# Where the last block of an MLP folds in the running maxima of the next image's scores

## The chip, the cores and the metric

One core of one Trainium2 chip runs the whole program in one launch. The metric is the device time of one execution in microseconds, median of the runs shown. Its engines are TensorE (PE in the profile; PEld is its weight load), VectorE (DVE), ScalarE (ACT), GpSimd (POOL) and SyncE (SP), each with its own instruction stream in order; they meet through semaphores.

## The reference

Four images of 256 channels by 64 x 64 pixels, all in fp32, pass through two layers. The first is an attention over the 4096 pixels of an image:

```python
q = jnp.einsum('oc,bcn->bno', wq, xf) + bq
k = jnp.einsum('oc,bcn->bon', wk, xf) + bk[None, :, None]
attn = jax.nn.softmax(jnp.einsum('bnd,bdm->bnm', q, k), axis=-1)
v = jnp.einsum('oc,bcn->bon', wv, xf) + bv[None, :, None]
out = jnp.einsum('bcn,bmn->bcm', v, attn).reshape(B, Cc, H, W)
return gamma[0] * out + x
```

The second normalizes the result, adds the output of a small clustering step, normalizes again, adds an MLP (256 to 1024 channels, tanh-GELU, back to 256), and ends in a channel scale and a 256 x 256 pointwise convolution, each with batch norm and ReLU.

## The kernel before

The order of instructions is the order of the Python calls: `tc.manual_schedule()` keeps each engine's stream as written, and the framework adds only the semaphore waits that data and buffers need. The four images run one after another, and each goes through `weighting` (the attention's sums, about half a thousand microseconds), `cluster`, and `mlp`. The beginning of the next image's attention is woven into the present image's `cluster` and `mlp`.

**Scores of the next image.** A block of attention is 512 query pixels. Its scores are made in eight units of 512 keys, `score(u)` at L351: four matmuls of 32 rows each (L364) write two PSUM halves, two ScalarE copies (L372 and L373) put them into an SBUF tile `s`, and the softmax needs the maximum over all of it. For the units made inside the MLP the maxima are not recorded on the spot. `score` appends them to a list, `maxima`, as four closures (unit 0: two), each of which records one VectorE instruction when it is called, L377: `top = max(top, s quarter)`, 128 x 512. The first two of a unit read what L372 copied, the other two what L373 copied.

**The MLP's blocks.** `mlp` walks over eight blocks of 512 pixels (seven for the third image, whose eighth block is done later by `late_block`). Each block has four steps, `j` = 0 to 3, one for each pair of 128-channel groups of the hidden layer. A step is one call of `first`, which calls `seven`: seven half-size products instead of eight, in three groups of PSUM banks, `hp`, `hq` and `hr` (all L1377), with additions on VectorE (L1368, through `plus`), one ScalarE copy (L1385) and four GELUs (L1332). The banks come from a pool of two, so a group reuses the bank of the group but one before it, once that has been read. Between these products TensorE does the second layer's products of the step before, `mo`: L1294 in all blocks but the last, and L1278 in the last, where `end` is true. `slots` says how many of them go at each of four places.

In the last block, VectorE also finishes the block before it: three additions L1436 to L1438 and updates of `x` at L1423, some of them called from `plus` through the list `drips`. ScalarE's two ReLUs L1414 follow, then GpSimd's L1222, and TensorE's pointwise products `pw` at L1233 in step 2. The helper `rest()` takes one closure out of `maxima`, if there is one, and records it; in every block it is called ahead of and behind `first` in steps 2 and 3. The table `at` places the score units: unit 6 behind step 3 of the last block but one and unit 7 behind step 2 of the last; for the third image, units 6 and 7 behind steps 1 and 2 of the last block.

**Behind the last block** comes the handover:

```python
        for _ in range(2):
            next(todo)
        if nxt:
            while maxima:
                rest()
            nxt.fold(0)
            nxt.maximum()
        table(AF.Exp)
        for _ in todo:
            pass
        if nxt:
            nxt.first()
```

Two `mo` products of step 3 are recorded; all maxima that are left are recorded; `fold` (L394) reduces `top` to one row of 512; `maximum` calls `across`, where TensorE transposes `top` (`tt`, L400), VectorE takes the row maxima (L402) and spreads them on a diagonal (`dg`, L404). Then the other two `mo` products follow, `first` spreads the maxima over PSUM with a matmul by ones (`mb`, L453), `finish` and `last` complete the block (L1423, L1414, `pw`), and the exponentials (L465, L468) and sums (`av`, L478) of the next image start. The fourth image has no next one, and its list is empty.

Of the kernel before, what the change touches and what calls it, by code (L numbers as in the profile page):

```python
# [45 lines left out]
def attention_then_cluster_block(  # L46
# [1114 lines left out]
    def mlp(b, ys, stats2, fill, nxt, blocks, turned, maxima):  # L1161
# [26 lines left out]
        def norm(nb, eng):  # L1188


            pairs[nb] = pr = spool.tile([P, 2, KC, NB], F32, tag="s", name=f"xn2_{b}_{nb}")

            def scaled(k):
                nc.vector.tensor_scalar(
                    pr[:, 0, k, :],
                    block(ys, k, nb),
                    ga[:, k : k + 1],
                    gb[:, k : k + 1],
                    ALU.mult,
                    ALU.add,  # L1200
                )

            def parts():
                rest = factors(eng, pr[:, 0], pr[:, 1])
                scaled(0)
                if nb == 0:
                    next(rest)
                scaled(1)
                yield
                yield from rest  # L1210

            rest = parts()
            next(rest)
            return rest
# [4 lines left out]
        def last(nb, beside, eng):  # L1219

            zs = pairs.pop(nb)
            eng.tensor_tensor(zs[:, 0, 1], zs[:, 1, 0], zs[:, 1, 1], ALU.subtract)  # L1222

            if beside:
                ps = [
                    ps_m.tile([P, NB], F32, tag="m", name=f"pw{c}_{b}_{nb}") for c in range(KC)
                ]
            else:
                two = ps_s.tile([P, 2, NB], F32, tag="s", name=f"pw_{b}_{nb}")
                ps = [two[:, c, :] for c in range(KC)]  # L1230
            for c in range(KC):
                for k in range(KC):
                    nc.tensor.matmul(  # L1233
                        ps[c],
                        pw_q[2 * k + c],
                        zs[:, 0, 1] if k and c else zs[:, 1, k],
                        start=(k == 0),
                        stop=(k == KC - 1),
                    )
            for c in range(KC):  # L1240
                rectified(c, zs[:, 0, c], ps[c])
                leave(nb, c, zs[:, 0, c])

        def rectified(c, o_s, src):
            nc.scalar.activation(
                o_s, src, AF.Relu, scale=pw_s[:, c : c + 1], bias=pw_e[:, c : c + 1]
            )

        def leave(nb, c, o_s):
            nc.sync.dma_start(out=ob[:, c, nb * NB : (nb + 1) * NB], in_=o_s)  # L1250

        def factors(eng, src, dst):


            e, f, g, h = quarters(src)
            t2, t4, t3, _ = quarters(dst)
            yield eng.tensor_tensor(f, f, e, ALU.subtract)
            yield eng.tensor_tensor(t2, h, f, ALU.subtract)
            yield eng.tensor_tensor(t3, e, t2, ALU.subtract)
            yield eng.tensor_tensor(t4, t2, g, ALU.subtract)  # L1260
# [65 lines left out]
        def first(nb, j, todo, slots, meanwhile=lambda: None):  # L1326


            hs = work.tile([P, 2, NB], F32, tag=("t", "acc")[j % 2], bufs=1, name=f"hs_{b}_{nb}_{j}")

            def gelu(i, src):
                nc.scalar.activation(  # L1332
                    src, src, AF.Gelu_apprx_tanh, bias=pvc("b1", P, j + 4 * (i > 1))
                )

            ws = [
                w[:, j * P : (j + 1) * P] for w in (W_A, w_abcd, W_CD, w_bac, w_bcd, W_B, W_D)
            ]
            seven(f"{nb}_{j}", ws, pairs[nb][:, 0], pairs[nb][:, 1], quarters(hs), gelu, todo, slots, meanwhile)
            return hs  # L1340
# [71 lines left out]
        def finish(nb, acc):  # L1412
            def relu(c):
                nc.scalar.activation(  # L1414
                    pairs[nb][:, 1, c, :],
                    block(ys, c, nb),
                    AF.Relu,
                    scale=dw_d[:, c : c + 1],
                    bias=dw_e[:, c : c + 1],
                )  # L1420

            def scaled(y, term, c):
                nc.vector.scalar_tensor_tensor(y, term, par("ls2", c), y, ALU.mult, ALU.add)  # L1423

            if len(acc) == KC:
                for c in range(KC):
                    scaled(block(ys, c, nb), acc[c], c)
                    relu(c)
                return

            _, _, z, w = acc
            p7, p5, p6, p4 = (t[:, i * HB : (i + 1) * HB] for t in (z, w) for i in range(2))
            own = pairs[nb][:, 1]
            d1, d2, d3, d4 = quarters(own)
            y0, y1 = block(ys, 0, nb), block(ys, 1, nb)
            nc.vector.tensor_tensor(d4, p6, d1, ALU.add)  # L1436
            nc.vector.tensor_tensor(d3, p7, d4, ALU.add)
            nc.vector.tensor_tensor(d2, p5, d4, ALU.add)  # L1438
            scaled(y1[:, HB:], p5, 1)
            scaled(y1[:, :HB], p4, 1)  # L1440
            drips.append(lambda: scaled(y0, own[:, 0], 0))
            drips.extend([lambda: None] * 3)
            drips.append(
                lambda: scaled(
                    y1.rearrange("p (x n) -> p x n", x=2),
                    d3.unsqueeze(1).to_broadcast([P, 2, HB]),
                    1,
                )
            )
            hooks.append(lambda: relu(0))  # L1450
            return lambda: relu(1)
# [9 lines left out]
        def rest():  # L1461
            if maxima:
                maxima.pop(0)()
# [8 lines left out]
        for nb in range(blocks):  # L1472
            end = nb == blocks - 1
            for j in range(4):
                if j > 1:
                    rest()
                pw = (lambda: last(nb - 1, True, nc.gpsimd)) if end and j == 2 else lambda: None
                hs = first(nb, j, todo, slots, pw)
                if nb == 0 and j == 0:
                    fill(N)  # L1480
                if j > 1:
                    rest()
                if j == 0:
                    if nb:
                        rectify = finish(nb - 1, acc)
                    acc = [
                        ps_a.tile([P, NB], F32, tag=f"a{c}", name=f"mo{c}_{b}_{nb}")
                        for c in range(KC)
                    ]
                    if not end:  # L1490
                        acc += [
                            ps_m.tile([P, NB], F32, tag="m", name=f"mo{c}_{b}_{nb}")
                            for c in range(2, 4)
                        ]
                    elif nxt:

                        nc.sync.dma_start(
                            out=a21_s, in_=w2.rearrange("(k p) m -> p k m", p=P)[:, :h_n, P:]
                        )
                        nxt.q_block(1, nc.sync)  # L1500
                elif j == 1:
                    assert not drips and not hooks
                    if nb:
                        rectify()
                    if not end:
                        ahead = norm(nb + 1, nc.gpsimd)
                        if nb:
                            own = factors(nc.gpsimd, pairs[nb - 1][:, 1], pairs[nb - 1][:, 0])
                        else:
                            own = left_factors()  # L1510
                elif j == 2 and nb and not end:
                    pointwise(nb - 1)
                scored = nxt and (nb, j) in at
                if scored:
                    copies = []
                    nxt.score(at[nb, j], copies, maxima)
                    copies.pop()()
                if len(acc) == KC:
                    todo = second(nb, acc, hs, j)
                    slots = (2, 1, 1, 0) if scored else (0, 1, 1, 2)  # L1520
                else:
                    todo = second_by_seven(nb, acc, hs, j, own, ahead)
                    slots = (0, 2, 2, 3)
                    if scored:
                        slots = (3, 1, 2, 1)
                    elif j == 2 and nb:
                        slots = (3, 1, 0, 3)
# [32 lines left out]
    with tc.manual_schedule():  # L1560
# [3 lines left out]
        for b in range(B):  # L1564
# [11 lines left out]
            stats, cells, rest = here.weighting(ahead, fill, (lambda: None) if b else derived)  # L1576
# [82 lines left out]
```

## Time and profile before

| what | value |
|---|---|
| median of 3 runs | 3349.32 us (3348.83 to 3349.82) |
| profiled execution, its own time | 3348.09 us |
| its span, first to last instruction | 3346.3 us |
| mean granted TensorE clock | 0.997 |
| VectorE busy | 2222.5 us (66%) |
| ScalarE busy | 1681.7 us (50%) |
| GpSimd busy | 1931.9 us (58%) |
| L377, maxima by closures: 120 instructions, median, longest | 0.68 us, 1.21 us |

The span lies 1.8 us under the profiled execution's own time, and that execution 1.2 us under the median. In a timeline row the first number is the start in microseconds from the beginning of the span, the second the length of the group, "x4" the number of instructions that were merged, and the bracket the engine's idle time ahead of it with the instruction that ended it. An fp32 matmul stands as two records, and a record's end is modelled with the pipeline's tail in it, so the next one can start some 0.16 us ahead of that end. Three places of the span matter here, the ends of the first three images' MLPs, at about 880, 1710 and 2513 us.

### The profile page before, as it was taken

To read this page: it belongs to the slowest core of one execution; us is meant where nothing else is said; L and a number is where in the kernel's file an instruction comes from. 1 tells how busy PE (TensorE), PEld (TensorE's weight loads), DVE (VectorE), ACT (ScalarE), POOL (GpSimd) and SP (SyncE) were. 2 spreads that over 40 slices of the span, in tenths; PEclk is the share of its full clock that TensorE was granted. 3 is DMA by queue.
4 is the path that set the end of the run, shared out by engine and by line. 5 is a ranking of instruction groups with operands and counts; after the bars stand their busy time and mean duration, and the time that the engine had idled before them with its cause. 6 is when DMAs were issued, how large, how long until landed. Compare 5 with 4: busy or idle time off the path is not lost.

```text
span 3346.3 us, 34677 instructions
## 1 busy us (share of the span) xinstructions
PE 3301.5 (99%) x12266; PEld 1805.9 (54%) x12266; DVE 2222.5 (66%) x3554; ACT 1681.7 (50%) x2253; POOL 1931.9 (58%) x1366
## 2 busy tenths in 40 slices
PE   8999999999999999999999999999999999999999
PEld 4433444788533344578844334457873343446786
DVE  5667764677666766467766676647766766765675
ACT  5545553545555554355455555435455555544444
POOL 2655666366365676646636566554644676573664
PEclk9999999999999999999999999999999999999999
DMA  2000002000000000200000000010000000010000
GB/s 72 13 13 10 14 9 87 4 13 20 26 12 13 13 13 16 78 4 20 20 23 13 10 13 13 23 71 4 20 26 13 13 13 13 10 40 1 13 20 26
DMA packets 43101, 70.97 MB, mean 21 GB/s; under 512 B 9680, under 2 KB 18480, under 8 KB 42928
## 3 DMA queue, kind: packets, MB, share of 16 engines
q1 hardware_dynamic: 37040, 60.83, 5.5%
q10 hardware_dynamic: 5632, 7.41, 0.9%
q8 instruction: 96, 1.57, 0.2%
q0 software_dynamic: 256, 0.52, 0.1%
q14 instruction: 77, 0.63, 0.1%
HBM read 43.46 MB, written 16.89 MB: 18 GB/s over the span
## 4 chain that ended last, share of the span: by engine, by line
PE 94%; DVE 4%; ACT 1%; POOL 1%; DMA 0%; issue 0%; ACTq 0%; DVEq 0%; POOLq 0%
PE av L478 54%; PE mo L1294 9%; PE sc L364 8%; PE hq L1377 5%; PE hp L1377 3%; PE hr L1377 3%; PE fv L874 3%; PE vp L315 2%; PE mo L1278 1%; PE hq_pw L1377 1%; DVE st L979 1%; PE pw L1233 1%; PE hr_pw L1377 1%; PE hp_pw L1377 1%; DVE x L998 0%; DVE top L377 0%
## 5 line engine op out<-in xcount | busy, mean ns | idle before, releaser
L478 PE MATMUL av<-s,v 128*128 128x512 f32 x4096 | 1819.2, 598 | 0.6 <-ACT s L468 0.6
L473 POOL TENSOR_TENSOR acc<-acc,s 128x1024 f32<-128x1024 f32 x448 | 1057.7, 2361 | 538.4 <-ACT s L468 519.5
L478 PEld LDWEIGHTS av<-s,v 128*128 128x128 f32 x4096 | 759.1, 190 | 1044.7 <-issue 1034.5
L468 ACT ACTIVATE s<-s 128x1024 f32<-128x1024 f32 x512 | 540.1, 1057 | 592.5 <-DVE s L465 549.5
L465 DVE TENSOR_TENSOR s<-s,mb 128x1024 f32<-128x1024 f32 x512 | 595.9, 1206 | 19.0 <-ACT mb L449 16.4
L386 DVE TENSOR_TENSOR top<-sc,top 128x1024 f32<-128x1024 f32 x196 | 239.5, 1222 | 374.7 <-PE sc L364 374.4
L1332 ACT ACTIVATE hs<-hs,pv_s 128x256 f32<-128x256 f32 x496 | 232.4, 502 | 340.7 <-DVE hs L1368 340.7
L1294 PE MATMUL mo<-hs,w 128*128 128x256 f32 x1512 | 387.0, 382 | 0.0
L382 ACT COPY s<-sc 128x1024 f32<-128x1024 f32 x224 | 224.9, 1004 | 225.5 <-PE sc L364 225.5
L1294 PEld LDWEIGHTS mo<-hs,w 128*128 128x128 f32 x1512 | 282.5, 190 | 57.8 <-ACT hs L1332 19.8
L364 PE MATMUL sc<-q,k 32*128 32x512 f32 x2048 | 300.5, 640 | 0.4 <-ACT s L387 0.4
L389 DVE TENSOR_TENSOR top<-sc,top 128x1024 f32<-128x1024 f32 x196 | 240.1, 1225 | 71.9 <-ACT s L382 59.5
L387 ACT COPY s<-sc 128x1024 f32<-128x1024 f32 x224 | 227.1, 1014 | 66.4 <-DVE top L384 36.1
L1368 DVE TENSOR_TENSOR hs<-hq,hs 128x256 f32<-128x256 f32 x496 | 198.8, 422 | 78.3 <-PE hq L1377 68.4
L470 POOL TENSOR_TENSOR acc<-s 128x1024 f32<-128x1024 f32 x32 | 75.3, 2353 | 285.0 <-ACT s L468 285.0
L1301 POOL TENSOR_TENSOR hs<-hs 128x256 f32<-128x256 f32 x108 | 82.3, 762 | 189.2 <-ACT hs L1385 85.1
L364 PEld LDWEIGHTS sc<-q,k 32*128 32x128 f32 x2048 | 86.4, 182 | 183.7 <-issue 123.1
L1368 DVE TENSOR_TENSOR hs<-hp,hs 128x256 f32<-128x256 f32 x124 | 52.2, 421 | 136.5 <-ACT hs L1385 136.5
L315 PE MATMUL vp<-wv_s,x 128*128 128x256 f32 x512 | 127.8, 395 | 1.9 <-ACT v L323 1.5
L1377 PE MATMUL hr<-xn,w 128*128 128x256 f32 x496 | 127.5, 379 | 0.5 <-DVE hs L1368 0.5
L315 PEld LDWEIGHTS vp<-wv_s,x 128*128 128x128 f32 x512 | 95.1, 194 | 30.2 <-issue 12.7
L1377 PEld LDWEIGHTS hr<-xn,w 128*128 128x128 f32 x496 | 94.1, 190 | 19.1 <-issue 4.8
(262 smaller groups left out, 3495.5 us busy)
## 6 DMA issues: line engine op xcount, KB each, us to landing
out<-xn SPq DMA_DIRECT2D x62, 256.0 KB, 2.1
x<-in_x SPq DMA_DIRECT2D x30, 512.0 KB, 6.5
w<-in_w SPq DMA_DIRECT2D x8, 1024.0 KB, 10.2
mr<-row_mx SPq DMA_DIRECT2D x28, 256.0 KB, 3.1
rden<-row_rd SPq DMA_DIRECT2D x28, 256.0 KB, 3.1
q<-q ACTq DMA_DIRECT2D x96, 64.0 KB, 2.0
mix<-in_wfv SPq DMA_DIRECT2D x8, 192.0 KB, 8.1
q<-q SPq DMA_DIRECT2D x24, 64.0 KB, 2.0
```

Of the source, the lines that this page charges most:

```text
L315: nc.tensor.matmul(vps[0][:, i % 2, :], xs[i * P // XT][:, k, o : o + P], wv_s[:, k, :], start=(k == 0), stop=(k == KC - 1),)
L364: nc.tensor.matmul(halves[r // 2][:, r % 2, :], k_s[rows, g, :], q_s[rows, :], start=True, stop=True)
L386: nc.vector.tensor_tensor(top, halves[1], top, ALU.max)
L389: nc.vector.tensor_tensor(top, halves[0], top, ALU.max)
L465: nc.vector.tensor_tensor(sh, sh, mxs[nb].unsqueeze(1).to_broadcast([P, 2, NB]), ALU.subtract)
L468: nc.scalar.activation(sh, sh, AF.Exp)
L473: nc.gpsimd.tensor_tensor(acc, acc, s[:, 2 * h : 2 * h + 2], ALU.add)
L478: nc.tensor.matmul(av[c], own["v"][:, RG * g + quarter, c * P : (c + 1) * P], slots[u][:, quarter, :], start=(g == 0 and quarter == 0), st ...
L1294: return nc.tensor.matmul(bank[:, half * HB : (half + 1) * HB], a[:, j], t, start=start, stop=stop)
L1332: nc.scalar.activation(src, src, AF.Gelu_apprx_tanh, bias=pvc("b1", P, j + 4 * (i > 1)))
L1368: nc.vector.tensor_tensor(dst, ps, term, ALU.add)
L1377: nc.tensor.matmul(out, w, x, start=True, stop=True)
```

## The change

Two edits in the loop over the steps of `mlp`, both for the last block alone (`end`): `rest()` is also called behind `first` in steps 0 and 1, and twice more ahead of `first` in step 3.

```diff
             for j in range(4):
                 if j > 1:
                     rest()
+                if end and j == 3:
+
+                    rest()
+                    rest()
                 pw = (lambda: last(nb - 1, True, nc.gpsimd)) if end and j == 2 else lambda: None
                 hs = first(nb, j, todo, slots, pw)
                 if nb == 0 and j == 0:
                     fill(N)
-                if j > 1:
+                if j > 1 or end:
                     rest()
```

Four more closures are thus taken out of `maxima` ahead of the handover's `while maxima` loop. Lines behind the edits move down by four.

## The prediction

> **What bounds the kernel now.** I read the page first. Its first line and the chain of waits say that TensorE sets the time:
>
> ```profile
> PE 3301.5 (99%) x12266; PEld 1805.9 (54%) x12266; DVE 2222.5 (66%) x3554; ACT 1681.7 (50%) x2253; POOL 1931.9 (58%) x1366
> ...
> PE 94%; DVE 4%; ACT 1%; POOL 1%; DMA 0%; issue 0%; ACTq 0%; DVEq 0%; POOLq 0%
> ```
>
> So an edit to VectorE's order pays only where TensorE stands idle for VectorE, or runs slowly because it stood idle. I then read TensorE's timeline at the ends of the first three images' MLPs. These are the first end and the third; the second equals the first to within 0.02 us (`tt` at 1710.10, idle 1.54):
>
> ```profile
> 877.90 1.98 PE L1278 MATMUL mo<-hs,w 128*128 128x512 f32 x4 [1.06 <-ACT hs L1332]
> 881.43 0.66 PE L400 MATMUL tt<-ident,top 128*128 128x128 f32 x4 [1.54 <-DVE top L394]
> ...
> 2507.90 1.98 PE L1278 MATMUL mo<-hs,w 128*128 128x512 f32 x4 [1.06 <-ACT hs L1332]
> 2513.83 0.66 PE L400 MATMUL tt<-ident,top 128*128 128x128 f32 x4 [3.95 <-DVE top L394]
> 2514.32 2.81 PE L1278 MATMUL mo<-hs,w 128*128 128x512 f32 x4
> ```
>
> The transposes `tt` wait for `fold`, L394: 1.54 us twice and 3.95 us once. VectorE's timeline at the same ends says why: behind the last additions of step 3 stand five maxima (nine for the third image) and then the fold. The last two rows are from step 2 to 3 of the first image:
>
> ```profile
> 877.55 3.09 DVE L377 TENSOR_TENSOR top<-top,s 128x512 f32<-128x512 f32 x5
> 880.68 0.69 DVE L394 TENSOR_TENSOR top<-top 128x512 f32<-128x512 f32 x1
> ...
> 2507.55 5.50 DVE L377 TENSOR_TENSOR top<-top,s 128x512 f32<-128x512 f32 x9
> ...
> 868.11 1.28 DVE L377 TENSOR_TENSOR top<-top,s 128x512 f32<-128x512 f32 x2
> 873.41 0.42 DVE L1368 TENSOR_TENSOR hs<-hp,hs 128x256 f32<-128x256 f32 x1 [4.01 <-ACT hs L1385]
> ```
>
> Ahead of step 3's additions VectorE idles 4.01 us. Last, the granted clock (the number behind POOL's) in short windows:
>
> ```profile
> 640.00:660.00 20.00, 18.52 (x82) 14.62 (x82) 14.18 (x36) 9.61 (x18) 9.80 (x11) 0.91 0.00 1
> ...
> 880.00:884.00 4.00, 2.57 (x9) 1.37 (x10) 3.18 (x6) 0.00 (x0) 0.00 (x0) 1.00 0.00 0
> ...
> 2514.00:2516.00 2.00, 2.00 (x7) 1.04 (x7) 1.44 (x3) 0.00 (x0) 0.00 (x0) 0.78 0.00 0
> 2516.00:2518.00 2.00, 2.00 (x4) 0.89 (x3) 1.35 (x2) 0.85 (x2) 0.00 (x0) 0.50 0.00 0
> 2518.00:2520.00 2.00, 2.00 (x5) 0.81 (x5) 1.20 (x2) 0.78 (x1) 0.00 (x0) 0.86 0.00 0
> ```
>
> After the third end's 3.95 us of idling TensorE worked about 3.4 us at half clock; after the first end's 1.54 us it did not.
>
> **What moves.** Nothing is added or removed: in the built programs only VectorE's order differs, and no other stream, wait or DMA moves. Counting closures (unit 6 leaves four at the start of the last block, unit 5 for the third image):
>
> - first and second image, before: one maximum ahead of step 2, two between steps 2 and 3, five behind step 3. After: one behind step 0, two between 1 and 2, one of unit 6 and three of unit 7 between 2 and 3, one behind step 3.
> - third image, behind step 3: nine before, five after; the three new ones ahead of step 3 are of unit 6.
>
> One more maximum in a row costs (3.09 - 0.68)/4 = 0.60 us, and (5.50 - 3.09)/4 = 0.60 us again.
>
> **Gain at the first two ends.** Four maxima less bring the fold forward by 2.41 us, from 881.37 to 878.96. TensorE's four `mo` records, from 877.90, let the next matmul start after 1.82 us (as in step 2: `mo` at 870.12, `hp` at 871.94), at 879.72. That is later than the fold, so TensorE becomes the limit: `tt` moves from 881.43 to 879.72, a gain of 1.71, not of 2.41. What follows hangs on `tt` (L402, `dg`, `mb`, L1423, L1414, `pw`) and moves with it: 1.7 each. What is late next is the 1.06 us wait for the GELU ahead of these `mo` records, which stays.
>
> **Gain at the third end.** Nine minus five maxima is again 2.41 us; here the fold remains the last to come, so `tt` moves by all of it and idles 1.54, the picture that the first end shows today. From the start of `tt` to the first `av` the first end takes 888.74 - 881.43 = 7.31 us and the third 2522.77 - 2513.83 = 8.94. With idle time shortened to 1.54 the half clock should go, worth 1.63. Here the Trainium skill, "TensorE: Matmul & The Clock Gate", section "Part 1: The HAM clock gate", has a rule: the clock halves after a whole idle window of about 3.4 us, counted freely. By it 1.54 us can't halve the clock, and 1.63 is certain. The trace is less kind: between 640 and 660 us the clock was halved (mean 0.91) where the longest idle piece is 1.44 us, with one-column matmuls around it. So the rule's threshold is too high for this kernel. I still take 1.63, from the nearest rows, two ends with 1.06 and 1.54 us idle at clock 1.00; the other bound, 0, I give a chance. Sum 4.04.
>
> **Cost of the early places.** The maximum behind step 0 falls into a stretch in which VectorE has no gap (852.35 to 859.51), so everything there slips by 0.60: L1436 to L1438, L1423, the additions of step 1, and ScalarE's GELUs and ReLUs behind them.
>
> ```profile
> 852.35 0.76 DVE L1368 TENSOR_TENSOR hs<-hr,hs 128x256 f32<-128x256 f32 x2
> 853.02 0.41 DVE L1436 TENSOR_TENSOR xn<-mo,xn 128x256 f32<-128x256 f32 x1
> ...
> 858.74 0.89 ACT L1332 ACTIVATE hs<-hs,pv_s 128x256 f32<-128x256 f32 x2
> ...
> 860.41 1.27 POOL L1222 TENSOR_TENSOR xn<-xn 128x512 f32<-128x512 f32 x1 [9.98 <-ACT xn L1414]
> ```
>
> Who waits: `mo` at 859.93 reads the GELU of 858.74, which ends at 859.25 and after the slip at 859.85. With some 0.05 for a semaphore its weights load about 0.15 later than now, of which overlap leaves 0.05 on TensorE. `hr` needs the `hp` addition read out: 855.34 before, 855.94 after, weights at 856.06: free by 0.1. L1222 slips to 861.0 and ends by 862.3; its reader is the last pair of the `pw` that starts at 862.94: hidden. The two maxima ahead of step 2 end at 860.7, and the addition behind them, 860.62 now, goes to 861.24 with its copy L1385; the next one waits for `hq` until 862.29 anyway (1.24 idle). For the third image unit 6's `sc` at 2486.99 takes its second half's bank from step 1's `hr` additions, read out at 2486.74, after the slip at 2487.34; that half starts 0.39 later, and TensorE with it, as when the same wait stretched unit 7's `sc` to 2.04 us at 2498.14. Total: 0.05, 0.05, 0.39. Without the slacks of 0.1 to 1.2 named here, each end would lose up to the 0.60.
>
> **Cost of the places ahead of step 3.** VectorE runs in order: a maximum that waits for unit 7's copies holds step 3's additions behind it. The copies L372 and L373 end at 871.28 and 872.20; two maxima start at 871.32, the third at 872.52 and ends at 873.20. The addition behind it starts at 873.41: free by 0.2, and even if late, 1.32 us of idle time ahead of `hq`'s addition covers it. In the third image unit 6 is copied long before; three maxima run from 2499.5 to 2501.4, the addition comes at 2503.41.
>
> A second rule speaks against the change: the skill's "GPSIMD Engine Reference", section "1. Specifications", says that GpSimd shares its SBUF interfaces with VectorE and contends with VectorE instructions with two SBUF inputs, which these maxima are. The trace agrees that they can stretch: one beside L1260 took 0.95, the longest 1.21. By the rule alone four moved maxima at 0.95 would cost 3.8 us of VectorE instead of 2.4. But GpSimd is idle from 850.4 to 860.4 and from 861.7 to 888.3, so I take 0.60.
>
> **Sum.** 1.71 - 0.05 twice, and 4.04 - 0.39: 3.3 + 3.65 = 7.0 us, call it 7.1 with the 0.02 to 0.03 that the unstalled `tt` saves at the first two ends. The profiled execution, 3348.09, would become 3341.0. It lies 1.2 under the median, so the prediction is 3349.32 - 7.1 = 3342.2. TensorE is bound by `av` behind each end, with hundreds of microseconds of its own work, so no transfer can take the time back. About 0.2% (6.7 us) is what a measurement can tell from no change, and 7.1 lies barely beyond it. The half-clock windows around the second group norm of each image can fall differently once everything is earlier: the stretch 3098 to 3120 has a mean clock of 0.77, and I allow 1 us either way for it.
>
> **Rivals.**
>
> 1. *The half clock stays at the third end.* For: it appears after 1.44 us of idling near 640. Against: it doesn't at 880 and 1710. Gain 7.1 - 1.63 = 5.5: 3343.8. Chance 0.13.
> 2. *The early slip is passed on, so that the maxima come back elsewhere.* If none of the slacks holds, 0.60 is lost at each early place and up to three times 0.60 ahead of step 3, 2.4 per end for a gain of 1.7 to 4.0; half of that is 3.6 lost: 3345.8; all of it, no change. For: the stretch without a gap. Against: idle rows of 4.01, 1.32 and 1.24. Chance 0.15.
> 3. *Slower: the moved maxima lie on the path at their longest.* Place: the four new places of each end; price 1.21 each, 4 x 1.21 x 3 = 14.5, less 7.5 gained (1.71 twice and 4.04): 3356.3. It decides from the point where VectorE has no idle time there and GpSimd runs beside; net loss begins at 0.63 us lost per moved maximum. Against: both conditions fail in the trace. Chance 0.03.
> 4. *More is gained*, if a group norm's half-clock window disappears as well: 3340.5. Chance 0.07.
>
> That the change doesn't do what it says is excluded by the built order.
>
> **Numbers.** The forecast has 0.62, with 3342.2 and its own range 3341.0 to 3343.5. Range 3340.3 to 3345.8: it takes in rivals 1 and 4 and the half of rival 2. Faster by over 0.2% means under 3342.6: about 0.8 of the forecast's cases and rival 4, 0.57. Slower 0.03. Within 0.2%: 0.40.
>
> **What would show it.** Right: one L377 (five at the third end) behind step 3; `tt` without idle time at the first two ends and with 1.54 at the third; clock 1.00 there; `sc` of unit 6 longer by 0.4 in the third image; step 1's `mo` within 0.1 of its place. Wrong: idle time at `hp`, `hq` or `mo` in steps 1 to 3, L377 longer than 0.7, or a clock of 0.5 behind the third `tt`.

## The result, and the profile after

The changed kernel takes 3341.33 us (median of 13 runs, 3339.96 to 3341.83) against 3349.06 us for the kernel before (13 runs beside it): 7.7 us less, ratio 0.9977 with a 95% interval of 0.9969 to 0.9984. A later series on another occasion gave 3341.10 against 3348.85. The profiled executions differ by 6.6 us (3341.48 against 3348.09).

TensorE's timeline at the first and the third end, in the kernel after:

```profile
877.86 1.98 PE L1278 MATMUL mo<-hs,w 128*128 128x512 f32 x4 [1.06 <-ACT hs L1332]
879.68 0.60 PE L400 MATMUL tt<-ident,top 128*128 128x128 f32 x4
...
2505.10 1.98 PE L1278 MATMUL mo<-hs,w 128*128 128x512 f32 x4 [1.06 <-ACT hs L1332]
2508.62 0.66 PE L400 MATMUL tt<-ident,top 128*128 128x128 f32 x4 [1.54 <-DVE top L394]
2509.11 1.88 PE L1278 MATMUL mo<-hs,w 128*128 128x512 f32 x4
```

The first row of `tt` has no bracket any more, the third end's bracket has gone from 3.95 to 1.54 us, and the `mo` group behind it takes 1.88 us instead of 2.81. VectorE's rows around step 3 of the first image and behind step 3 of the third:

```profile
868.07 0.68 DVE L377 TENSOR_TENSOR top<-top,s 128x512 f32<-128x512 f32 x1
871.27 1.90 DVE L377 TENSOR_TENSOR top<-top,s 128x512 f32<-128x512 f32 x3 [2.52 <-ACT s L372]
873.37 0.42 DVE L1368 TENSOR_TENSOR hs<-hp,hs 128x256 f32<-128x256 f32 x1 [0.20 <-ACT hs L1385]
...
877.51 0.68 DVE L377 TENSOR_TENSOR top<-top,s 128x512 f32<-128x512 f32 x1
878.23 0.69 DVE L394 TENSOR_TENSOR top<-top 128x512 f32<-128x512 f32 x1
...
2504.75 3.09 DVE L377 TENSOR_TENSOR top<-top,s 128x512 f32<-128x512 f32 x5
```

The three maxima ahead of step 3 wait for the copy L372, as worked out, and still leave 0.20 us ahead of step 3's first addition. The granted clock behind the third `tt`:

```profile
2508.00:2510.00 2.00, 1.38 (x7) 0.90 (x8) 1.25 (x2) 0.00 (x0) 0.00 (x0) 1.00 0.00 0
2510.00:2512.00 2.00, 1.91 (x5) 0.46 (x3) 1.97 (x5) 0.52 (x1) 0.00 (x0) 1.00 0.00 0
```

Each end can be measured locally, from the last `sc` in the block before (unit 6's, or unit 5's for the third image) to the first `av` of the next image, so that nothing earlier or later enters:

| end | before | after | difference | predicted |
|---|---|---|---|---|
| first | 845.04 to 888.74: 43.70 us | 844.94 to 886.93: 41.99 us | -1.71 | -1.7 |
| second | 1673.71 to 1717.41: 43.70 us | 1672.17 to 1714.16: 41.99 us | -1.71 | -1.7 |
| third | 2472.87 to 2522.77: 49.90 us | 2469.68 to 2515.93: 46.25 us | -3.65 | -3.65 |

The first `av` behind the third end, in the profile before and in the profile after:

```profile
2522.77 3.60 PE L478 MATMUL av<-s,v 128*128 128x512 f32 x8
...
2515.93 3.60 PE L478 MATMUL av<-s,v 128*128 128x512 f32 x8
```

The ends give 7.07 us in these two executions. The spans differ by 6.6; the other 0.5 us is lost in the stretches outside, whose code is the same and in which the half clock falls differently from one execution to the next. The largest such difference is behind the third end: from that `av` to the end, the nine profiles of this document take 823.5 to 824.7 us; the four over 824.4 have 13.7 us at half clock around the fourth image's group norm, the five under 823.8 have 6.8 or 10.2. It is 10.2 in the profiles before and after: from 3080 to 3130 us their mean clock is 0.90.

### The profile page after: what moved, and what is told of

The parts are those of the page before. It is cut to its first block, busy times and chain, and to the rows that moved or that the text cites. A ratio compares the mean times of both kernels' runs of the same rounds, so it can differ in the third digit from the quotient of the medians.

```text
span 3339.7 us, 34679 instructions
## 1 busy us (share of the span) xinstructions
PE 3301.1 (99%) x12266; PEld 1805.5 (54%) x12266; DVE 2221.2 (67%) x3554; ACT 1682.1 (50%) x2253; POOL 1931.4 (58%) x1366
## 3 DMA queue, kind: packets, MB, share of 16 engines
q8 instruction: 96, 1.57, 0.2%
## 4 chain that ended last, share of the span: by engine, by line
PE 95%; DVE 3%; ACT 1%; POOL 1%; issue 0%; DMA 0%; ACTq 0%; DVEq 0%; POOLq 0%
PE av L478 54%; PE mo L1294 10%; PE sc L364 8%; PE hq L1377 5%; PE hp L1377 3%; PE hr L1377 3%; PE fv L874 3%; PE vp L315 2%; PE mo L1278 1%; PE hq_pw L1377 1%; DVE st L979 1%; PE pw L1233 1%; PE hr_pw L1377 1%; PE hp_pw L1377 1%; DVE x L998 0%; PE qp L334 0%
```

## The experiments

All times below are medians beside the kernel before on the same chip: 3349.32 us (59 runs) for the first four, 3348.85 us (23 runs) for the last three. The changed kernel was timed in the first series (3341.33 beside 3349.06) and with the last three, not with the first four; a difference of 1 or 2 us from it is less than the intervals can tell, so the profiles decide there.

**The first two images alone.**

```diff
-                if end and j == 3:
+                if end and blocks == NBLK and j == 3:
...
-                if j > 1 or end:
+                if j > 1 or (end and blocks == NBLK):
```

> The new places for the first and second image alone; the third image's last block as before. If each end pays by its own idle time (theory): 1.7 us at each of the first two ends, none at the third: about 3349.1 - 3.4 = 3345.7 us, tt without idle time twice and 3.95 us idle with half clock at the third end. If the gain comes from the third end alone (rival: the half clock was all that mattered): 3349 us.

Measured: 3345.86 us, 3.5 us less; ratio 0.9990 (0.9982 to 0.9998). The first two `tt` start without idle time. The third end is that of the kernel before, in its code and in its 3.95 us of idle time. But its clock isn't that of the profile before:

```profile
2508.00:2510.00 2.00, 0.00 (x0) 0.00 (x0) 1.97 (x5) 0.00 (x0) 0.00 (x0) 0.75 0.00 0
2510.00:2512.00 2.00, 1.36 (x5) 1.25 (x6) 0.79 (x2) 0.00 (x0) 0.00 (x0) 0.50 0.00 0
2512.00:2514.00 2.00, 2.00 (x3) 0.67 (x2) 1.84 (x3) 0.04 (x1) 0.00 (x0) 0.50 0.00 0
2514.00:2516.00 2.00, 2.00 (x4) 0.86 (x3) 0.75 (x1) 0.77 (x2) 0.00 (x0) 0.54 0.00 0
```

A mean of 0.75 over 2 us is 1 us at half clock, so the four rows hold 1.0 + 2 + 2 + 1.8 = 6.8 us of it, twice what the profile before had (0.78, 0.50 and 0.86: 0.9 + 2 + 0.6 = 3.4). On 5.2 us of it TensorE was working (1.4, 2.0 and 1.8 in the last three rows), and at half clock that takes about 2.6 us more than at full clock. From `tt` to the first `av` it took 2520.43 - 2510.64 = 9.79 us, against 8.94 in the profile before and 7.3 at full clock. The same wait thus costs 1.6 us in one execution and 2.5 in another.

**The third image alone.** The same edits with `blocks < NBLK` in place of `blocks == NBLK`.

> The new places for the third image alone. Theory: 2.41 us of idle time less, 1.63 us for the half clock, 0.39 us lost in the score products of unit 6: 3349.1 - 3.65 = 3345.4 us, clock 1.00 behind tt. If the half clock has nothing to do with the idle time (rival), it stays: 2.0 us, 3347.1 us. The sum of the gains of this kernel and of the one with the first two images alone should be the whole 7 to 7.7 us, if the ends don't act on each other.

Measured: 3344.52 us, 4.8 us less; ratio 0.9986 (0.9980 to 0.9993). Its profile shows 1.54 us of waiting for `tt` and 7.31 us from there to `av` (2512.03 to 2519.34), and the whole third end takes 46.25 us as in the changed kernel, so the mechanism is the predicted one; the gain in the medians is 1.1 us more than predicted. With 2.48 us for the half clock, as in the kernel above, instead of 1.63, 4.5 us would be expected. The two parts add to 8.3 us, near the whole of 7.7: the ends don't act on each other to any extent that these medians show.

**Without the place behind step 0.**

```diff
-                if j > 1 or end:
+                if j > 1 or (end and j == 1):
```

> The changed kernel without the place behind step 0. Theory: at the first two ends the one maximum more behind step 3 lies in the 0.7 us by which the fold was early, and the 0.05 us lost in step 1 comes back: no change there. Third end: the wait for tt grows by 0.60 to 2.14 us, and unit 6's score products are short again, 0.39 us less: +0.2. Together 3341.3 to 3341.7 us. If the slip behind step 0 costs its full 0.60 us at each end (rival), this kernel gains: 1.2 at the first two ends, 3340.1 us or less.

Measured: 3342.54 us, ratio 0.9980 (0.9973 to 0.9988), about 1 us more than the changed kernel: more than expected. The two counted steps held. At the first two ends `tt` still starts without idle time; unit 6's `sc` in the third image is back at 1.14 us, and the third end waits 2.14 us. What I had not expected is in the clock:

```profile
2508.37 0.65 PE L400 MATMUL tt<-ident,top 128*128 128x128 f32 x4 [2.14 <-DVE top L394]
2508.86 3.56 PE L1278 MATMUL mo<-hs,w 128*128 128x512 f32 x4
...
2508.00:2510.00 2.00, 1.63 (x6) 1.12 (x7) 1.22 (x3) 0.00 (x0) 0.00 (x0) 0.73 0.00 0
2510.00:2512.00 2.00, 2.00 (x3) 0.67 (x2) 1.14 (x2) 0.77 (x1) 0.00 (x0) 0.50 0.00 0
```

(The first two rows are from the timeline, the last two from the windows.) In this execution 2.14 us of idle time were enough to halve the clock: `tt` to `av` is 2517.31 - 2508.37 = 8.94 us again. The whole third end takes 48.10 us (from 2469.21), 1.85 more than in the changed kernel. So the place behind step 0 is worth more in the third image than its 0.6 us: with it the wait is 1.54 us and the clock stays. It seems that 2.14 us do not halve it in every execution: five of the 15 runs took 3340.8 to 3341.3 us, as the changed kernel does, with mean clocks of 0.997 and 0.998, while five of the six over 3343 us had 0.996. Only one of them was profiled, so this is not shown.

**Three maxima behind step 0** in the first two images:

```diff
                 if j > 1 or end:
                     rest()
+                if end and j == 0 and blocks == NBLK:
+                    rest()
+                    rest()
```

> The changed kernel with three maxima behind step 0 for the first and second image instead of one (the two between steps 1 and 2 become one, the two around step 2 and the first of the four ahead of step 3 find no unit 6 left; the number behind step 3 stays one). VectorE slips by 1.81 us instead of 0.60. Theory: the slack of mo in step 1 is 0.55 us, all beyond it lands on TensorE: about 1.25 us lost per image, 2.4 us more than the changed kernel, 3343.7 us; tt still without idle time. Rival: the idle times of 1.2 and 4.0 us that VectorE has later in the block absorb the slip: 3341.3 us.

Measured: 3343.69 us, ratio 0.9984 (0.9977 to 0.9990), 2.4 us over the changed kernel (2.1 by the gains, each beside its own kernel before), where 2.4 were expected. Step 1 and the start of step 2 in TensorE's timeline show the two waits that take the time:

```profile
856.34 1.13 PE L1377 MATMUL hr<-xn,w 128*128 128x256 f32 x4 [0.55 <-DVE hs L1368]
...
860.23 1.12 PE L1278 MATMUL mo<-hs,w 128*128 128x512 f32 x2 [0.18 <-ACT hs L1332]
```

From step 1's `hp` to step 2's `hq` it takes 861.19 - 851.72 = 9.47 us, in the changed kernel 860.75 - 852.49 = 8.26: 1.21 us per image. `hr` waits for the bank that VectorE's `hp` addition reads out late, and `mo` for a GELU, the two waits named in the prediction. VectorE's later idle time doesn't give this back.

**No wait at the third end either.** No place behind step 0; three maxima more ahead of step 3 in the first two images; in the third, five more ahead of step 2 and two more ahead of step 3:

```diff
                 if end and j == 3:
-
-                    rest()
-                    rest()
+                    for _ in range(2 if blocks < NBLK else 3):
+                        rest()
+                if end and j == 2 and blocks < NBLK:
+                    for _ in range(5):
+                        rest()
...
-                if j > 1 or end:
+                if j > 1 or (end and j == 1):
```

> No place behind step 0. First and second image: three more places ahead of step 3 instead of two (one maximum behind step 3, as in the changed kernel). Third image: six places ahead of step 2 instead of one and three ahead of step 3, so that one maximum is left behind step 3 instead of five. Theory: first two ends as in the changed kernel, with the 0.05 us of step 1 back; third end: tt without idle time, 1.7 us less than in the changed kernel, unit 6's score products short again, 0.39 us less: 3341.3 - 2.2 = 3339.1 us, which beats both kernels. Rival: maxima that wait for unit 6's or 7's copies hold the additions of step 2 or 3 behind them, hq or hr get idle time, and it is 3341 us or more.

Measured: 3338.68 us (6 runs), ratio 0.9970 (0.9958 to 0.9981) to the kernel before, 2.4 us under the changed kernel beside it; it is the fastest of all. VectorE and TensorE in the third image:

```profile
2482.53 5.36 DVE L377 TENSOR_TENSOR top<-top,s 128x512 f32<-128x512 f32 x7
2487.82 0.41 DVE L1368 TENSOR_TENSOR hs<-hp,hs 128x256 f32<-128x256 f32 x1
2488.98 1.67 DVE L1368 TENSOR_TENSOR hs<-hq,hs 128x256 f32<-128x256 f32 x4 [0.75 <-PE hq L1377]
...
2505.60 0.60 PE L400 MATMUL tt<-ident,top 128*128 128x128 f32 x4
```

Seven maxima fill the gap ahead of step 2's additions, the additions for `hq` still wait 0.75 us for TensorE, and `tt` starts without idle time at all three ends. The maxima hold an addition back, but not one that TensorE needs. The third end takes 44.11 us (2468.74 to 2512.85) against 46.25 in the changed kernel: 2.1 us less, as expected. One of the seven maxima took 1.75 us, while GpSimd's L1222 ran:

```profile
2484.11 1.43 POOL L1222 TENSOR_TENSOR xn<-xn 128x512 f32<-128x512 f32 x1 [9.99 <-ACT xn L1414]
...
2484.33 1.75 DVE L377 TENSOR_TENSOR top<-top,s 128x512 f32<-128x512 f32 x1
```

That is more than the 1.21 us that rival 3 priced, and it cost nothing there because VectorE had the time.

**A busy wait.** The kernel before, with matmuls whose result nobody reads in the third end's wait:

```diff
         for _ in range(2):
             next(todo)
+        if nxt and blocks < NBLK:
+            busy = ps_s.tile([P, 2, NB], F32, tag="s", name=f"busy_{b}")
+            for i in range(4):
+                nc.tensor.matmul(
+                    busy[:, i % 2, :], w2_s[:, 0, :P], hs[:, 0], start=True, stop=True
+                )
```

> The kernel before, with four matmuls more (128x512, 0.86 us each, their result is not used) behind the first two mo products of the third image's last step, in the time in which TensorE waits for the fold: 3.45 us of the 3.95 us of idle time are filled. No maximum is moved. Theory: tt starts when it did, but the clock behind it stays at 1.00, and from tt to the first av it takes 7.3 us instead of 8.9 to 9.8: 1.6 to 2.5 us less than before, 3347.2 us. If the half clock has another cause than TensorE's idle time (rival): 3349.3 us, clock 0.5 behind tt.

Measured: 3346.41 us, 2.4 us less; ratio 0.9992 (0.9984 to 1.0000). The interval reaches 1, but all 13 runs (3345.73 to 3347.10) lie under all 23 of the kernel before (3347.81 to 3350.44). Four needless matmuls make the kernel faster, though no maximum moves:

```profile
2509.83 3.60 PE L1533 MATMUL busy<-hs,w 128*128 128x512 f32 x8
2513.94 0.66 PE L400 MATMUL tt<-ident,top 128*128 128x128 f32 x4 [0.51 <-DVE top L394]
2514.43 1.88 PE L1278 MATMUL mo<-hs,w 128*128 128x512 f32 x4
...
2514.00:2516.00 2.00, 2.00 (x8) 1.00 (x8) 1.34 (x3) 0.00 (x0) 0.00 (x0) 1.00 0.00 0
2516.00:2518.00 2.00, 1.57 (x4) 0.59 (x4) 2.00 (x4) 1.21 (x2) 0.00 (x0) 1.00 0.00 0
```

(Three rows of the timeline, two of the windows.) `tt` stands where it stood, the clock behind it is 1.00, and `tt` to `av` takes 2521.24 - 2513.94 = 7.30 us. This isolates the half clock as a price of idling, 2.4 us in the medians, and shows that it isn't tied to anything that the moved maxima do.

**The changed kernel again**, beside the last two.

> The changed kernel itself, beside the other two on one chip, for direct comparison: 3341.3 us as before, 0.15% over the kernel without the wait at the third end if that one does what its theory says.

Measured: 3341.10 us, ratio 0.9977 (0.9968 to 0.9986). Its profile repeats the three ends of the profile after: 41.99, 41.99 and 46.25 us.

## Why the prediction was right, point by point

- *TensorE becomes the limit at the first two ends, 1.7 us each.* Shown by the local difference of 1.71 and by the first experiment, 3.5 us for both. The fold is early there (it ends at 878.92, `tt` starts at 879.68), and one maximum more behind step 3 changes nothing, as the kernel without the place behind step 0 shows.
- *2.41 us of waiting less at the third end.* 3.95 to 1.54, exactly.
- *The half clock goes with the wait, 1.63 us.* The cause is shown by the busy wait. The size is the term of the sum that was too small: 1.63 came from one execution that held 3.4 us of half clock, while the same wait in another held 6.8 us and cost 2.48, and the medians of the busy wait say 2.4. Put into the sum, 2.4 gives 7.9 us instead of 7.1, and 7.7 were measured. How much of these medians comes from the third end, and how much from the half clock around the fourth image's group norm, which moves a run by about 1 us, is not separated: the kernel before was profiled once. That the table's third row matches to 0.01 us is no evidence for 1.63 as the usual cost, since the forecast and the row use the same profile before.
- *Cost of the early places, 0.05, 0.05 and 0.39.* VectorE slipped by 0.60, and where it was to land it did: unit 6's score products in the third image, 1.14 us before, are stretched by 0.39, and step 1's `mo` in the first image by 0.06 (1.08 against 1.02). One slack was read too small: `hr` was given 0.1 us, counted to the load of its weights. In the changed kernel the `hp` addition ends at 855.84 and `hr` starts at 856.39; with three maxima behind step 0 they stand at 856.28 and 856.34. So some 0.5 us were left, which changes nothing in the sum.

```profile
859.84 1.08 PE L1278 MATMUL mo<-hs,w 128*128 128x512 f32 x2
...
2483.80 1.53 PE L364 MATMUL sc<-q,k 32*128 32x512 f32 x8
```

- *Slack decides what a slip costs.* Tripled, it cost 1.21 us per image, against 1.25 worked out from the 0.55 us of slack at `mo`. That speaks against rival 2; and rival 3 needed maxima at 1.21 us, while those moved took 0.60 to 0.68 each with GpSimd idle beside them. The one of 1.75 us in the fastest kernel shows that this hangs on the place.
- *Rival 1, the half clock stays*, was closer than its chance said: 1.54 us idle keeps the clock, 2.14 us lost it in the execution that was profiled. The prediction doubted the rule of the Trainium skill ("TensorE: Matmul & The Clock Gate", Part 1: The HAM clock gate) that a whole idle window of 3.4 us is needed, and rightly: by it 2.14 us would have kept the clock. With 0.6 us more behind step 3 the forecast for this end would have been 1.6 us too good by that profile.
- *Rival 4, a group norm's half clock goes as well*, is not seen in the profile after, as the mean clock of 0.90 there shows.

The forecast of 7.1 us lay only just beyond the 6.7 us that the prediction took as the least that can be told from no change. With the half clock left in place, 5.5 us, it would have been below.

## What to carry to other kernels

When TensorE sets the time, look at how long it idles, and at the granted clock behind that: the wait of 3.95 us here cost about half as much again afterwards, and taking the last part of it away may be worth more than its length. A maximum, copy or sum that isn't needed yet belongs where its engine idles ahead of an instruction that waits anyway; its price there is the slip less the slack of the first reader that TensorE waits for, and here that reader was twice a bank to be reused (`hr` in step 1, unit 6's `sc`) and once data (`mo`). If the wait can't be removed, useless matmuls in it can keep the clock up, as four did here.

## What the runs showed of the hardware

The clock was halved after 2.14 us of idle time in one piece (with another 1.06 us that ended 2 us earlier), in the one profile that has it, and not after 1.54 us (with the same 1.06), at the third end of four profiles. It came in pieces of 3.4 us, one or two of them for one wait of 3.95 us, in executions of the same instructions. I had taken its cost as one number; it was 1.6 us in one profile and 2.5 in another, and four matmuls without use, 3.45 us long, took it to nothing.

The length of the wait alone doesn't decide. If each profile is cut into stretches of 3.41 us, with borders at which half clock begins somewhere in it, TensorE was busy for 1.31 us in the stretch just ahead of the half clock in the profile before (2511.73 to 2515.14), for 1.27 without the place behind step 0, and for 1.09 with the first two images alone. The clock stayed full after a stretch with 1.57 us busy (2508.31 to 2511.73 in the profile before, the earlier part of the same wait) and after one with 1.87 (2505.55 to 2508.96 in the profile after, whose half clock began at 645.28, 546 stretches ahead of 2508.96). So it seems to count how much TensorE works in such a stretch, and a border that cuts a wait in two can save the clock. This is worked out from these profiles; no run was built to test it, and two stretches don't fit a single limit. With the first two images alone, 1.78 us of work at half clock (2509.01 to 2512.42) were followed by half clock again; and in the profile before 1.97 us (641.22 to 644.63), part of them one-column matmuls, were followed by the half clock that the prediction saw near 640.
